# The last stage of a two-layer graph network: stores on ScalarE's queue, ten batches of x loaded ahead, statistics joined from parts

## The chip, the cores and the metric

The kernel runs on one core of a Trainium2 chip. The metric is the device time of one execution in microseconds (us), the median of three runs. A core has five engines that work side by side: TensorE (PE in the profile, with PEld for its weight loads), VectorE (DVE), ScalarE (ACT), GpSimd (POOL) and SyncE (SP). Each of them runs its own list of instructions in order, and they wait for one another by semaphores. Transfers between the device memory and the on-chip memory (DMAs) are issued by an engine and then run by themselves.

## The reference

Two layers with a residual each; everything is float32. There are 16 batches of 1024 nodes with 256 features.

```python
h = maximum(layernorm(x), 0)
x = x + layer0(h, para, adj, kv_w)      # graph weights, then attention with 4 heads
h = maximum(layernorm(x), 0)
x = x + layer1(h, adj, W1, b1, g1, be1, W2, b2, g2, be2)

def layer1(features, A, W1, b1, g1, be1, W2, b2, g2, be2):
    A_hat = (A + I) normalised by its degrees
    x   = (A_hat @ features).reshape(-1, 256)
    h   = relu(batchnorm(x @ W1.T + b1, g1, be1))   # 512 features
    out = batchnorm(h @ W2.T + b2, g2, be2)         # 256 features
    return out.reshape(16, 1024, 256)

def batchnorm(x, gamma, beta):                      # over all 16384 rows
    return (x - mean(x, 0)) * rsqrt(var(x, 0) + 1e-5) * gamma + beta
```

What matters here is the end. The second batch normalisation needs the mean and the variance of each of 256 features over all 16384 rows. So the last products have to be done, and their statistics joined, before the first value of the output can be scaled.

## The kernel before

There are two stages. Stage one does layer 0 and the first half of layer 1, batch by batch. It leaves two things in device memory: `x1_d`, the residual x of every batch, and `z1_d`, the 512 features before the first batch normalisation, as 32 tiles of 512 rows. Stage two starts at L985 and is what the change is about. It has three parts.

1. **Second linear layer (L1155 to L1243).** Each of the 32 tiles of z1 is fetched by SP (`fetch`, L145), scaled and cut at zero on ACT (`relu_on`, L134), and multiplied by W2 on PE into two blocks c of 128 features. Tiles 2 to 25 are done in pairs with seven products (`Pair`), the others plainly. The result z2 stays on chip, with the features on partitions. DVE takes the statistics of every 128x512 block with `bn_stats` into `st2` (six numbers for each block and feature). The last two tiles (30 and 31) stay in PSUM, in the four tiles of `ps_last`, and the order there is c = 0 for both tiles, then c = 1 for both.
2. **The second batch normalisation (`bn2`, L110 to L129).** `invert` joins the 32 records of a block with `bn_aggr`, adds eps on DVE, takes the power -1/2 on POOL, and adds b2 to the mean and takes it away again; `affine` makes from this the scale s and the shift t for each feature.
3. **The output loop (L1269 to L1291).** For each batch, z2 is scaled by s and t (`finish`: ACT does c = 0, DVE does c = 1), turned by 16 transposes on PE into two PSUM tiles of 128x4x256 (`ps_out` holds two), added on DVE to x of that batch (two instructions of 128x1024 at L1288), and stored (two DMAs of 512 KB, issued by POOL at L1289). The scaling of batch b+1 stands before the two additions of batch b.

The residual x comes back in two halves for each batch (`load_x1`, on SP's queue). `AHEAD = 9` batches are asked for before the loop. Batches 0 to 6 go into the pool `io`, which has 14 buffers of 4 KB per partition that the tiles of the pairs used before (tag `x1`); batches 7 and 8 go into the four buffers that hold the fetched z1 tiles 30 and 31 (pool `lasting`, tag `z`), and so have to wait for the last products. Batch b+9 is asked for at the end of turn b, into the buffers of a batch that has been stored; such a load waits for that store to land.

The order of the instructions on each engine is the order of the program (`tc.manual_schedule`). A DMA that reuses a completion semaphore waits for the earlier DMA on it; there are eight of them for the DMAs of SP and eight for those of POOL.

`st1`, the statistics of the first batch normalisation, lies in a pool that lives to the end (`const`, L90). It is read for the last time at the end of stage one (`bn1.invert(2, 4)`, L771).

Of the kernel before, what the change touches and what calls it, by code (L numbers as in the profile page):

```python
# [10 lines left out]
F32 = mybir.dt.float32  # L11
# [13 lines left out]
AHEAD = 9  # L25
# [4 lines left out]
def fast_path(  # L30
# [59 lines left out]
    st1 = const.tile([P, FC, TT, 6], F32, tag="st1", name="f_st1")  # L90
# [7 lines left out]
    class BatchNorm:  # L98
# [11 lines left out]
        def invert(self, f0, f1):  # L110
            for f in range(f0, f1):
                nc.vector.bn_aggr(
                    self.mv[:, f, :], self.st[:, f, :, :].rearrange("p t s -> p (t s)")
                )
            at = slice(f0, f1)
            nc.vector.tensor_scalar_add(self.var[:, at], self.mv[:, at, 1], EPS)
            nc.gpsimd.tensor_tensor(
                self.rstd[:, at], self.var[:, at], mhalf[:, : f1 - f0], ALU.pow
            )
            if self.offset is not None:  # L120
                mean = self.mv[:, at, 0]
                nc.vector.tensor_add(mean, mean, self.offset[:, at])
                nc.vector.tensor_sub(mean, mean, self.offset[:, at])

        def affine(self, f0, f1):
            at = slice(f0, f1)
            nc.vector.tensor_mul(self.s[:, at], self.rstd[:, at], self.gamma[:, at])
            nc.vector.tensor_mul(self.ms[:, at], self.mv[:, at, 0], self.s[:, at])
            nc.vector.tensor_sub(self.t[:, at], self.beta[:, at], self.ms[:, at])  # L129

    bn1 = BatchNorm(st1, FC, g1_t, be1_t, "bn1")
# [24 lines left out]
    with ExitStack() as stage:  # L156
# [8 lines left out]
        small = stage.enter_context(tc.tile_pool(name="fsmall", bufs=2))  # L165

# [818 lines left out]
    with ExitStack() as stage:  # L985
        big = stage.enter_context(tc.tile_pool(name="fbig2", bufs=1))
        io = stage.enter_context(tc.tile_pool(name="fio", bufs=NH * (AHEAD - 2)))

        xts = {}

        def load_x1(b, pool=None, tag="x1", bufs=None):

            xts[b] = []
            for h in range(NH):
                t = (pool or io).tile([P, NC // NH, C], F32, tag=tag, name=f"f_x1t_{b}_{h}", bufs=bufs)
                nc.sync.dma_start(t, x1_d[b].rearrange("(p h i) d -> p h i d", h=NH, p=P)[:, h])
                xts[b].append(t)

        st2 = big.tile([P, CC, TT, 6], F32, tag="st2", name="f_st2")
        with tc.manual_schedule(engines={ENG.PE, ENG.Activation, ENG.DVE, ENG.Pool, ENG.SP}):  # L1000
# [174 lines left out]
            for p in SEVEN:  # L1175
# [20 lines left out]
                else:  # L1196
# [5 lines left out]
                    for n in range(AHEAD - 2):  # L1202
                        load_x1(n)
# [14 lines left out]
                if p == SEVEN[1]:  # L1218
                    flag_out(bad)
            for n, t in enumerate(rest):  # L1220
# [12 lines left out]
            for t in range(TT - 2, TT):  # L1233
                relu_all(t)
            for c in range(CC):
                for t in range(TT - 2, TT):
                    ps = ps_last.tile([P, 512], F32, tag="last", name=f"f_z2ps_{t}_{c}")
                    product(ps, t, c, 0)
                    product(ps, t, c, 2)
                    nc.vector.bn_stats(st2[:, c, t, :], ps)  # L1240
                    last[t % 2, c] = ps
                bn2.invert(c, c + 1)
                bn2.affine(c, c + 1)  # L1243

            for b in range(AHEAD - 2, AHEAD):
                load_x1(b, lasting, "z", 4)
            ready = {}

            def finish(b, c, i0, i1):
                s, t = bn2.s[:, c : c + 1], bn2.t[:, c : c + 1]  # L1250

                def scaled(out, src):
                    if c == 0:
                        nc.scalar.activation(out, src, AF.Identity, bias=t, scale=s)
                    else:
                        nc.vector.tensor_scalar(out, src, s, t, ALU.mult, ALU.add)

                if b + 1 < B:
                    ready[b, c] = z2[:, c, b, :]
                    at = ready[b, c][:, i0 * P : i1 * P]  # L1260
                    scaled(at, at)
                else:
                    ready[b, c] = lasting.tile(
                        [P, N], F32, tag=("w2n", "w2T")[c], name=f"f_zo_{c}"
                    )
                    for g in range(NH):
                        scaled(ready[b, c][:, ts(g, 512)], last[g, c])

            for b in range(B):  # L1269
                xt = xts.pop(b)  # L1270
                out_v = out[b].rearrange("(p i) d -> p i d", i=NC)
                outs = []
                for i0 in range(0, NC, 4):
                    ps = ps_out.tile([P, 4, C], F32, tag="out", name=f"f_outps_{b}_{i0}")
                    for c in range(CC):
                        if b == 0:
                            finish(b, c, i0, i0 + 4)
                        for i in range(4):
                            nc.tensor.transpose(
                                ps[:, i, ts(c, P)], ready[b, c][:, ts(i0 + i, P)], ident  # L1280
                            )
                    outs.append(ps)
                if b + 1 < B:
                    for c in range(CC):
                        finish(b + 1, c, 0, NC)
                for i0, ps in zip(range(0, NC, 4), outs):
                    here = xt[i0 // 4]
                    nc.vector.tensor_add(here, here, ps)  # L1288
                    nc.gpsimd.dma_start(out_v[:, i0 : i0 + 4, :], here)  # L1289
# [516 lines left out]
```

## Time and profile before

| what | us |
|---|---|
| median of 3 runs (2463.08 to 2463.96) | 2463.73 |
| the profiled execution's own time | 2463.73 |
| its span, first to last instruction | 2461.9 |
| PE busy in the span | 2399.5 (97%) |
| DVE busy | 1700.3 (69%) |
| ACT busy | 1308.5 (53%) |
| last product of the second linear layer ends | about 2386.3 |
| first addition of the output loop starts | 2391.3 |
| first store is issued | 2393.2 |
| last addition ends | 2440.8 |
| last store is issued | 2447.2 |

The span is 1.8 us shorter than the time of the same execution; the difference lies around the program. All times in this document that have no other name are counted from the start of the span. The page of the whole execution shows PE busy throughout, up to the last fortieth of it or so; the part that the change touches is the last 75 us, with a few microseconds around 2185, where stage one goes over into stage two. The page's chain of waits is empty in this profile, so the end has to be read from the timelines of the single engines and from tables of windows.

In a line of the timeline stand the start, the duration, the engine, the line of the source, the operation with what it writes and reads, its shape, the number of instructions that are merged, and in brackets the idle time before it and what ended it. In a table of windows stand, for each stretch, the busy time of each engine, the clock that TensorE was granted (1.00 is full), the busy share of the DMA engines and the rate in GB/s.

### The profile page before, as it was taken

To read this page: it belongs to the slowest core of one execution; us is meant where nothing else is said; L and a number is where in the kernel's file an instruction comes from. 1 tells how busy PE (TensorE), PEld (TensorE's weight loads), DVE (VectorE), ACT (ScalarE), POOL (GpSimd) and SP (SyncE) were. 2 spreads that over 40 slices of the span, in tenths; PEclk is the share of its full clock that TensorE was granted. 3 is DMA by queue.
4 is the path that set the end of the run, shared out by engine and by line. 5 is a ranking of instruction groups with operands and counts; after the bars stand their busy time and mean duration, and the time that the engine had idled before them with its cause. 6 is when DMAs were issued, how large, how long until landed. Compare 5 with 4: busy or idle time off the path is not lost.

```text
span 2461.9 us, 24485 instructions
## 1 busy us (share of the span) xinstructions
PE 2399.5 (97%) x8062; PEld 1058.3 (43%) x8062; DVE 1700.3 (69%) x2314; ACT 1308.5 (53%) x1887; POOL 325.8 (13%) x577
## 2 busy tenths in 40 slices
PE   7999999999999999999999999999999999999984
PEld 4443444434343434444443434343444434444443
DVE  4787668584949486776859494958577586657746
ACT  7746546464646454554546364645555456246550
POOL 2030202020020302020202002030202020000002
PEclk9999999999999999999999999999999999999998
DMA  5041414222321414142322233241414220445559
GB/s 180 4 142 60 145 60 127 79 87 70 114 90 61 137 60 146 60 137 68 120 75 91 75 100 97 67 139 60 146 60 137 69 65 31 159 174 174 190 194 365
DMA packets 174424, 271.82 MB, mean 110 GB/s; under 512 B 37584, under 2 KB 121040, under 8 KB 174288
## 3 DMA queue, kind: packets, MB, share of 16 engines
q1 hardware_dynamic: 154128, 237.62, 29.7%
q0 software_dynamic: 20160, 32.55, 4.2%
q8 instruction: 66, 1.08, 0.2%
q14 instruction: 70, 0.57, 0.1%
HBM read 165.68 MB, written 70.84 MB: 96 GB/s over the span
## 4 chain that ended last, share of the span: by engine, by line


## 5 line engine op out<-in xcount | busy, mean ns | idle before, releaser
L371 ACT ACTIVATE f_p<-f_s 128x1024 f32<-128x1024 f32 x512 | 477.4, 1046 | 155.4 <-PE f_s L363 155.3
L380 DVE TENSOR_TENSOR f_acc<-f_acc,f_p 128x1024 f32<-128x1024 f32 x384 | 470.5, 1225 | 42.1 <-DVE f_acc L380 1.8
L363 PE MATMUL f_s<-f_qT,f_kT 64*128 64x512 f32 x2048 | 456.9, 596 | 0.0
L404 PE MATMUL f_o<-f_p,f_v 128*64 128x512 f32 x2048 | 453.6, 595 | 0.0
L309 PE MATMUL f_gps<-f_w,f_h_a 128*128 128x512 f32 x1024 | 446.4, 596 | 3.8 <-DVE f_w L267 3.8
L286 POOL DMA_DIRECT2D f_hT<-f_hQ x480 | 236.4, 500 | 1221.3 <-PE f_gps L309 1172.0
L363 PEld LDWEIGHTS f_s<-f_qT,f_kT 64*128 64x128 f32 x2048 | 190.6, 185 | 263.4 <-ACT f_p L371 117.2
L309 PEld LDWEIGHTS f_gps<-f_w,f_h_a 128*128 128x128 f32 x1024 | 193.4, 191 | 253.0 <-issue 231.1
L404 PEld LDWEIGHTS f_o<-f_p,f_v 128*64 128x64 f32 x2048 | 141.4, 137 | 304.4 <-issue 256.2
L267 DVE SCALAR_TENSOR_TENSOR f_w<-f_w,f_adj 128x1024 f32<-128x1024 f32 x128 | 155.0, 1213 | 54.1 <-ACT f_w L266 54.1
L263 ACT ACTIVATE f_w<-f_row,f_col 128x1024 f32<-128x1024 f32 x128 | 148.1, 1157 | 24.9 <-DMA f_row<-frow 22.1
L220 ACT ACTIVATE f_h_b<-f_x,f_shift_b,f_rstd_b 128x256 f32<-128x256 f32 x128 | 64.6, 587 | 161.5 <-DVE f_shift_b L215 161.5
L266 ACT ACTIVATE f_w<-f_w 128x1024 f32<-128x1024 f32 x128 | 135.3, 1057 | 4.1
L595 DVE TENSOR_TENSOR f_aggT<-f_u,f_aps 128x512 f32<-128x512 f32 x16 | 11.0, 688 | 182.8 <-PE f_aps L552 182.8
L552 PE MATMUL f_aps<-f_ahatT,f_hs 128*128 128x512 f32 x256 | 115.1, 592 | 0.0
L327 PE MATMUL f_kps<-f_hT,f_kvw 128*128 128x512 f32 x256 | 113.5, 593 | 1.0 <-DVE f_qT L336 0.8
L552 PE MATMUL f_aps<-f_t,f_hs 128*128 128x512 f32 x256 | 112.6, 592 | 1.6 <-DVE f_hs L546 1.6
L342 PE MATMUL f_vps<-f_kvw,f_hT 128*128 128x256 f32 x512 | 113.1, 379 | 0.0
L552 PE MATMUL f_aps<-f_ahatT,f_h_b 128*128 128x512 f32 x256 | 112.6, 592 | 0.0
L342 PEld LDWEIGHTS f_vps<-f_kvw,f_hT 128*128 128x128 f32 x512 | 97.3, 190 | 20.1 <-issue 6.0
L220 ACT ACTIVATE f_h_a<-f_x,f_shift_a,f_rstd_a 128x256 f32<-128x256 f32 x128 | 75.0, 587 | 54.4 <-DVE f_shift_a L215 54.4
L377 DVE TENSOR_TENSOR f_acc<-f_p,f_p 128x1024 f32<-128x1024 f32 x64 | 76.3, 1192 | 29.9 <-ACT f_p L371 29.9
(181 smaller groups left out, 2563.8 us busy)
## 6 DMA issues: line engine op xcount, KB each, us to landing
f_t<-ft SPq DMA_DIRECT2D x84, 512.0 KB, 7.6
f_x<-in_x_dram SPq DMA_DIRECT2D x32, 1024.0 KB, 6.0
fz<-f_z SPq DMA_DIRECT2D x64, 512.0 KB, 9.2
f_zb<-fz SPq DMA_DIRECT2D x36, 512.0 KB, 5.6
f_para<-in_L_gnn_para_dram SPq DMA_DIRECT2D x32, 512.0 KB, 4.6
f_att<-f_oT SPq DMA_DIRECT2D x512, 32.0 KB, 1.9
fx<-f_x SPq DMA_DIRECT2D x16, 1024.0 KB, 5.6
f_x1t<-fx SPq DMA_DIRECT2D x32, 512.0 KB, 6.3
```

The source lines that it names most:

```text
L220: nc.scalar.activation(self.h[:, c, :], self.xt[:, c, :], AF.Relu, bias=self.shift[:, c : c + 1], scale=self.rstd[:, c : c + 1], accum_out ...
L263: nc.scalar.activation(w, rows[b], AF.Abs, bias=cols[b][:, c : c + 1], scale=0.5 / C)
L266: nc.scalar.activation(w, w, AF.Tanh)
L267: nc.vector.scalar_tensor_tensor(w, w, 1.0, adj_t[c], ALU.subtract, ALU.mult)
L286: queue.dma_start(to[ts(k, 32), ts(a, 32 * NC)], t[ts(a, 32), k].rearrange("i c r -> i (c r)"),)
L309: nc.tensor.matmul(gps[d][:, ts(g, 512)], hs[b][:, c, ts(d, P)], w[:, ts(g, 512)], start=(c == 0), stop=(c == NC - 1),)
L342: nc.tensor.matmul(ps[:, i, :], hT[e][:, ts(c4 + i, P)], kvw_t[:, e, C : 2 * C], start=(e == 0), stop=(e == CC - 1),)
L363: nc.tensor.matmul(ps[:, e, :], kT[rows_e, pair, ts(m, P)], qT[rows_e, pair, ts(g, 512)], start=True, stop=True,)
L371: nc.scalar.activation(p, ps, AF.Exp)
L380: nc.vector.tensor_add(acc_of[s], acc_of[s], p)
L404: nc.tensor.matmul(o_of[s][e * HD : (e + 1) * HD, :], v[:, m, ts(2 * pair + e, HD)], p[:, e, :], start=(m == 0), stop=(m == NC - 1),)
L552: nc.tensor.matmul(ps, left[:, m, :], right(m), start=not more and m == 0, stop=(m == KH - 1), skip_group_check=more,)
```

## The change

Six edits, all for the end of the kernel.

- `AHEAD` is 10. The pool `io` has 15 buffers in place of 14. Batch 9 of x is asked for ahead of the loop over the last plain tiles, its first half into the buffer `w2n` (which held the sums of W2 that the pairs use), its second into `io`. Batches 7 and 8 go where they went before.
- `st1` moves from the lasting pool into stage one's own.
- For the last block (c = 1, tile 31) the product is done in two halves of 256 columns, with `bn_stats` on each, and the records of the other 31 blocks are joined ahead in two groups (`gather`), so that the last `bn_aggr` reads six triples (count, mean, sum of squares) and not 32 records.
- In `bn2`, the mean is made negative in the step that takes b2 away, and the shift comes from one instruction for each block (`scalar_tensor_tensor`) and not from two.
- In the output loop, scaling runs two batches ahead. ACT does c = 0 of every batch and c = 1 of every odd one; DVE does c = 1 of the even ones. For batch 0, the second block is scaled in halves, one on each engine. The last batch's scaled values go into `io`.
- The stores are issued by ACT's queue, each right behind its addition, and no longer by POOL's. In the built program the DMAs of ACT and SP now share one set of eight completion semaphores.

```diff
-AHEAD = 9
+AHEAD = 10
...
-        def invert(self, f0, f1):
+        def invert(self, f0, f1, triples=None):
             for f in range(f0, f1):
                 nc.vector.bn_aggr(
-                    self.mv[:, f, :], self.st[:, f, :, :].rearrange("p t s -> p (t s)")
+                    self.mv[:, f, :],
+                    self.st[:, f, :, :].rearrange("p t s -> p (t s)")
+                    if triples is None
+                    else triples,
                 )
...
-                nc.vector.tensor_sub(mean, mean, self.offset[:, at])
+                nc.vector.tensor_sub(mean, self.offset[:, at], mean)
...
+            if self.offset is not None:
+                for f in range(f0, f1):
+                    one = slice(f, f + 1)
+                    nc.vector.scalar_tensor_tensor(
+                        self.t[:, one], self.mv[:, f, 0:1], self.s[:, one],
+                        self.beta[:, one], ALU.mult, ALU.add,
+                    )
+                return
...
-        io = stage.enter_context(tc.tile_pool(name="fio", bufs=NH * (AHEAD - 2)))
+        io = stage.enter_context(tc.tile_pool(name="fio", bufs=NH * (AHEAD - 3) + 1))
...
+            load_x1(AHEAD - 1, [(lasting, "w2n", 1), (io, "x1", None)])
             for n, t in enumerate(rest):
...
+            triples = big.tile([P, 6, 3], F32, tag="triples", name="f_triples")
+            SPLIT = TT // 2
+            for k, n in enumerate((SPLIT, TT - 1 - SPLIT)):
+                nc.vector.memset(triples[:, k, 0:1], float(n * 512))
+            def gather(k, t0, t1):
+                nc.vector.bn_aggr(
+                    triples[:, k, 1:3],
+                    st2[:, CC - 1, t0:t1, :].rearrange("p t s -> p (t s)"),
+                )
+                one = triples[:, k, 2:3]
+                nc.vector.tensor_scalar_mul(one, one, float((t1 - t0) * 512))
+            gather(0, 0, SPLIT)
             for c in range(CC):
                 for t in range(TT - 2, TT):
                     ps = ps_last.tile([P, 512], F32, tag="last", name=f"f_z2ps_{t}_{c}")
...
+                    gather(1, SPLIT, TT - 1)
+                    for k in range(2):
+                        at = slice(256 * k, 256 * (k + 1))
+                        for f in range(FC):
+                            nc.tensor.matmul(ps[:, at], w2T[:, f, ts(c, P)],
+                                zs[t, f - f % 2][:, f % 2, at],
+                                start=(f == 0), stop=(f == FC - 1))
+                        nc.vector.bn_stats(
+                            triples[:, 2 + 2 * k : 4 + 2 * k, :].rearrange("p k s -> p (k s)"),
+                            ps[:, at])
...
             for b in range(B):
                 xt = xts.pop(b)
...
+                if b == 0:
+                    finish(0, 0)
+                    finish(1, 0)
+                    for h in range(NH):
+                        turn_out(0, h, 0, outs[h])
+                    ready[0, 1] = z2[:, 1, 0, :]
+                    for h in range(NH):
+                        at = ready[0, 1][:, ts(h, 512)]
+                        scaled(at, at, 1, h == 1)
+                    finish(1, 1)
+                    for h in range(NH):
+                        turn_out(0, h, 1, outs[h])
+                else:
+                    for h in range(NH):
+                        for c in range(CC):
+                            turn_out(b, h, c, outs[h])
+                soon = [(b + 2, c) for c in range(CC)] if b + 2 < B else []
+                for n in soon:
+                    if by_scalar(*n):
+                        finish(*n)
+                for h in range(NH):
+                    nc.vector.tensor_add(xt[h], xt[h], outs[h])
+                    nc.scalar.dma_start(out_v[:, 4 * h : 4 * h + 4, :], xt[h])
+                for n in soon:
+                    if not by_scalar(*n):
+                        finish(*n)
                 if b + AHEAD < B:
                     load_x1(b + AHEAD)
```

`turn_out` issues the four transposes of one half and one block; `scaled` and `finish` are as before, except for the engine that is chosen (`by_scalar(b, c)`: c == 0 or b odd).

## The prediction

> **What bounds the kernel now.** I read the windows of the last 100 us first, because the page's chain of waits is empty and PE's 97% says nothing of the end.
>
> ```profile
> 2370.00:2380.00 10.00, 9.17 (x22) 3.91 (x21) 3.82 (x6) 0.00 (x0) 0.00 (x0) 1.00 0.22 83
> 2380.00:2390.00 10.00, 6.78 (x19) 2.97 (x17) 5.83 (x18) 7.30 (x8) 1.10 (x2) 0.96 0.64 207
> 2390.00:2394.40 4.40, 4.22 (x20) 4.15 (x21) 3.89 (x6) 4.40 (x5) 0.61 (x1) 0.50 0.03 10
> 2394.40:2404.00 9.60, 7.63 (x54) 6.33 (x53) 9.39 (x10) 7.00 (x8) 2.42 (x5) 0.92 0.97 334
> 2404.00:2440.00 36.00, 24.12 (x183) 19.26 (x180) 34.74 (x36) 0.00 (x0) 11.14 (x21) 1.00 1.03 411
> 2440.00:2453.00 13.00, 0.00 (x0) 0.00 (x0) 0.78 (x1) 0.00 (x0) 3.20 (x6) 0.51 1.03 415
> 2453.00:2458.00 5.00, 0.00 (x0) 0.00 (x0) 0.00 (x0) 0.00 (x0) 0.00 (x0) 0.50 0.43 175
> 2458.00:2461.90 3.90, 0.00 (x0) 0.00 (x0) 0.00 (x0) 0.00 (x0) 0.00 (x0) 0.50 0.00 0
> ```
>
> The columns are the stretch, its length, the busy time of PE, PEld, DVE, ACT and POOL, the granted clock, the DMA share and GB/s. From 2404 to 2453 the transfers run at 411 to 415 GB/s, share 1.03, while all engines are done at 2440.8. So the output loop is bound by bytes, not by its additions. Ahead of it the transfers stand nearly idle (83, 207 and 10 GB/s), and after 2458 nothing moves. The end is therefore: first packet of a store, plus bytes over rate, plus what is lost at both edges, plus the closing.
>
> Second, DVE's timeline shows why the first store comes when it does.
>
> ```profile
> 2386.38 0.70 DVE L1240 BATCH_NORM_STATS2 f_st<-f_z2ps 128x6 f32<-128x512 f32 x1 [2.73 <-PE f_z2ps L1012]
> 2387.11 1.02 DVE L112 BATCH_NORM_AGGREGATE f_bn_mv<-f_st 128x2 f32<-128x192 f32 x1
> ...
> 2389.38 0.16 DVE L129 TENSOR_TENSOR f_bn_t<-f_be,f_bn_ms 128x1 f32<-128x1 f32 x1
> 2389.57 1.73 DVE L1256 TENSOR_SCALAR f_z<-f_z,f_bn_s,f_bn_t 128x512 f32<-128x512 f32 x3
> 2391.33 1.22 DVE L1288 TENSOR_TENSOR f_x1t<-f_x1t,f_outps 128x1024 f32<-128x1024 f32 x1
> ```
>
> The shift of c = 1 is ready at 2389.54, three scalings take DVE to 2391.3, and only then the first addition runs, to 2392.55. POOL's timeline and the rows of the closing lines come third.
>
> ```profile
> 2393.21 0.61 POOL L1289 DMA_DIRECT2D out_dram<-f_x1t  x1 [4.25 <-DVE f_x1t L1288]
> 2403.75 1.65 POOL L1289 DMA_DIRECT2D out_dram<-f_x1t  x3 [3.53 <-DVE f_x1t L1288]
> ```
>
> ```profile
> L1317 POOLq EVENT_SEMAPHORE  x5: 17/43/43, 2454.2 to 2457.2; - x5
> L1317 ACTq TENSOR_LOAD <-flag x1: 462/462/462, 2388.8 to 2388.8; - x1
> L1317 POOLq INC_SWDGE_SEM  x1: 862/862/862, 2457.3 to 2457.3; - x1
> ```
>
> ```profile
> L1801 POOLq DRAIN  x3: 46/107/2841, 2458.2 to 2461.6; - x3
> ```
>
> POOL issues 0.66 us after the addition has ended, and once sits 3.5 us. Its last semaphore of a store passes at 2457.2; then it alone goes through 0.86 and 2.84 us of closing instructions before the engines meet at 2461.1 and end at 2461.9.
>
> **The sum before.** Bytes from the first packet on are the rates by the lengths of the rows: 9.6 x 0.334 + 36 x 0.411 + 13 x 0.415 + 5 x 0.175 = 24.27 MB. At 411 GB/s that is 59.05 us. From 2394.4 to 2457.2 are 62.8, so 3.75 are lost: 1.8 in the row at 334 GB/s (9.6 x 77/411) and 1.95 at the ramp down and last landing. Closing: 4.7. This profiled execution took 2463.73, the median itself, so differences of the span can be taken from the median.
>
> **1. Statistics and the first store: -2.3.** The last bn_stats has 256 columns: 0.41 (the layer norm's 128x256 bn_stats, L205) for 0.70. The last bn_aggr reads 18 numbers: between 0.15 (L207, 6 numbers) and 1.02 (192 numbers); I take 0.2, the row that it is nearest to. One small instruction of 0.16 and its gap, 0.20, goes. The product in halves costs 8 x 0.221 (L342, 128x256) for 4 x 0.43, +0.05. The early joins (two aggregates of 96 and 90 numbers, about 0.55 each, two multiplications, two memsets) lie in DVE's idle stretches of 3.08 and 2.73 before the last statistics; without that cover they would cost 1.4. So the shift is ready 1.3 earlier, at 2388.3. Then one half's scaling (L1256 at 128x512, 0.55), a semaphore, four transposes (0.60 at full clock; I add 0.2 for a halved one) and the addition, from 2389.8 to 2391.0: 1.5 earlier. ACT's sequencer reached its flag load at 2388.8 while ACT's scalings ran to 2401.4, so it issues ahead of its engine and I let it issue at 2391.05 without POOL's 0.66. An SP store alone (L742) lands in 2.6, POOL's quickest in 3.0, so the first packet comes 0.2 sooner after its issue: 2392.1 for 2394.4. Were ACT to work off its three scalings first (0.8 + 1.1 + 1.1), the issue would be at 2391.4. Ends: -1.0 to -2.6.
>
> **2. The hole at the start: -1.3.** DVE then gives a batch (1.05 MB) each 2.35 us for two additions, plus 0.8 on every second: 0.38 MB/us, nearly the rate, and loads join when the first store has landed, 2.6 after its issue. I leave 0.5 of the 1.8 lost. Ends: 0 to -1.8.
>
> **3. Batch 9: -2.55.** Its 1.05 MB move to the 83 GB/s stretch: SP asks for it ahead of batches 7 and 8, and its second half needs the buffer of plain tile 29, freed at about 2371.6 where SP issued its last load of batch 6. 1.05/0.411 = 2.55. It is worth that only as long as the loop stays bound by bytes. DVE's work per batch falls from 2.98 to 2.7 on average, ACT's is 1.5 scalings of 1.13 and two issues of 0.35, 2.4; with a load the bytes need 5.1, alone 2.55. DVE is thus hidden while loads run and is slightly the longer in the last batches, covered by its lead.
>
> **4. The closing: -2.35.** POOL has no store to wait for, so its 0.86 and 2.84 pass long before. What follows the last landing is SP's: eight semaphores (0.5, as at 2439.5 to 2440.0), twelve more (0.8), and the meeting of the engines (0.8): about 2.35 with gaps, for 4.7. Ends: 0 (if POOL's drain stays last) to -3.
>
> **5. Where stage one ends: +0.6.** The fifteenth buffer and the moved `st1` shift addresses. In the changed SP queue the first load of the first pair, once issued at 2166.4, stands behind the last four stores of z1 and waits for them; the last is issued at 2181.4 and lands 2.6 later. Here the trace has no slack:
>
> ```profile
> 2191.45 1.52 ACT L137 ACTIVATE f_zb<-f_zb,f_bn_t,f_bn_s 128x512 f32<-128x512 f32 x2 [1.60 <-DMA f_zb<-fz]
> 2193.37 1.52 ACT L137 ACTIVATE f_zb<-f_zb,f_bn_t,f_bn_s 128x512 f32<-128x512 f32 x2 [0.41 <-DMA f_zb<-fz]
> ...
> 2194.92 1.23 DVE L1064 TENSOR_TENSOR f_zt<-f_zb,f_zb 128x1024 f32<-128x1024 f32 x1 [7.99 <-ACT f_zb L137]
> 2198.82 1.95 PE L1074 MATMUL f_zx<-f_zt,f_w2s 128*128 128x512 f32 x4
> ```
>
> ACT already waits for these loads, DVE for ACT, and PE's product at 2198.82 starts as DVE's sums end. Another 512 KB ahead of them is 1.25 us of transfers (up to 1.9 at the slower rates there), less its head start of 1.1. PE has no idle time to absorb it later. Ends: 0 to +1.9.
>
> **Waits added.** Each store on ACT waits for its addition and for the DMA that used its semaphore before: in the built order mostly the store two batches back, four at the end. Behind a held store stand the scalings of batch b+3, and PE's transposes behind those. But scaling is two batches ahead, and at least 2 MB of stores plus loads stay under way, 5 us of transfers, so no transfer waits for it.
>
> The sum is -2.3 - 1.3 - 2.55 - 2.35 + 0.6 = -7.9: **2455.8**.
>
> The Trainium skill (DMA: Bandwidth & Descriptors, Issuing engines are not separate DMA queues) speaks against the move of the stores: all issuers share the same 16 engines, and a second issuer saves only issue time. The rows agree on rate (411 mixed, 415 for POOL alone). By the rule alone, terms 2 and 4 would be nothing and the sum 2459.5; I keep them, since they are POOL's stall and POOL's closing, not bandwidth.
>
> **Rivals.**
> - *POOL's drain stays last.* The 2.84 us may follow the end of all stores, whoever issues them: 2455.8 + 2.35 = 2458.2. For it: it is the last thing in the trace. Against: it follows POOL's own 0.86 directly.
> - *The seam costs more.* If the pair's load also waits for PE, all four loads shift by a whole load and more: 1.9 and a second product late, 2457.1 to 2459.
> - *Batch 9 isn't early.* If its buffers come free only with the last products, term 3 is gone: 2458.3. Against: SP's last load of batch 6 went out at 2371.6.
> - *Slower: ACT's queue starves the stores.* If the shared semaphores let only one batch be under way, a pair of batches needs landing 2.6 + scalings 2.3 + transposes 2.1 + addition 1.2 = 8.2 for 5.1 us of bytes; over the last five pairs that is 3.1 x 5 = 15.5: 2471. It decides once fewer than about 0.9 MB (2 us) are in flight.
>
> **Chances.** Forecast 0.62 (its own range 2453.5 to 2457.8), drain 0.12, seam 0.10, batch 9 0.06, ACT starving 0.06, the rest unnamed. The range of 8 in 10 is 2453.0 to 2460.0: the low end has every term near its better bound, the high one two terms lost. This kernel's measurement can tell 0.2%, 4.9 us: below 2458.8 is faster. That holds for the forecast, most of the drain and batch 9 cases and half the seam: 0.80; within 0.12; slower 0.08.
>
> **What would show it.** First store issued by ACT near 2391 (plus the seam's delay), a rate above 400 GB/s from 2 us later without a break, no load of batch 9 after 2380, and under 3 us from the last landing to the end. At the seam, the idle time before PE's product at 2198.8 gives term 5. I am wrong if the rate falls below 390 with both hardware queues, if ACT's stores wait long on semaphores with DMA idle, or if the drain of 2.84 still ends the span.

## The result, and the profile after

The changed kernel takes 2458.47 us in the median of 17 runs (2456.13 to 2461.64), the kernel before 2463.96 in 17 runs beside them (2462.04 to 2468.91): a ratio of 0.9976, with a 95% interval of 0.9969 to 0.9983. So it is faster, by 5.5 us where 7.9 were forecast, and inside the range of 2453.0 to 2460.0. The profiled execution took 2456.69, with a span of 2454.9; that is 7.0 less than the span before.

The windows of the end of the changed kernel, with the columns as before:

```profile
2370.00:2380.00 10.00, 9.17 (x22) 3.85 (x21) 4.49 (x10) 0.00 (x0) 0.00 (x0) 1.00 0.36 127
2380.00:2387.00 7.00, 6.47 (x25) 4.21 (x24) 3.70 (x11) 2.37 (x2) 0.55 (x1) 1.00 0.48 147
2387.00:2392.00 5.00, 2.35 (x20) 1.88 (x18) 3.65 (x10) 2.96 (x3) 0.55 (x1) 1.00 0.61 215
2392.00:2404.00 12.00, 9.59 (x74) 7.67 (x73) 11.77 (x12) 7.36 (x7) 0.00 (x0) 1.00 0.91 329
2404.00:2440.00 36.00, 21.49 (x136) 17.97 (x135) 23.52 (x23) 16.12 (x15) 0.00 (x0) 0.81 1.03 418
2440.00:2446.00 6.00, 4.13 (x32) 3.26 (x31) 5.55 (x5) 1.13 (x2) 0.00 (x0) 1.00 1.03 419
2446.00:2453.00 7.00, 0.00 (x0) 0.00 (x0) 0.00 (x0) 0.00 (x0) 0.00 (x0) 0.65 0.60 241
2453.00:2455.00 2.00, 0.00 (x0) 0.00 (x0) 0.00 (x0) 0.00 (x0) 0.00 (x0) 0.50 0.00 0
```

The transfers still set the end: 418 GB/s from 2404 on, without a break. DVE and PE are less busy in that stretch than before, and this costs nothing. From 2370 to 2380 the rate is 127 and not 83: that is batch 9. The first 12 us of the stores are still at 329 GB/s; that hole was to close and did not. ACT issues the first store at 2391.59:

```profile
2391.59 1.47 ACTq L1359 DMA_DIRECT2D out_dram<-f_x1t  x2
```

To see where the 7.0 us came from, both profiled executions are cut at the same events (the first and last packet are those of the stores in the trace's DMA records):

| piece | before | after | difference | forecast |
|---|---|---|---|---|
| start to stage one's last product (PE) | 2166.11 | 2164.76 | -1.35 | 0 |
| from there to the first pair's product that reads DVE's sums | 32.71 | 33.91 | +1.20 | +0.6 |
| from there to the start of the last plain tiles' products | 173.55 | 173.55 | 0 | 0 |
| from there to the first addition of the output | 18.96 | 18.12 | -0.84 | -1.5 |
| first addition to first packet of a store | 3.07 | 2.13 | -0.94 | -0.8 |
| first to last packet | 62.21 | 59.70 | -2.51 | -1.3 - 2.55 |
| last packet to end of the span | 5.29 | 2.73 | -2.56 | -2.35 |

Of what the change touches, only the place of `st1` lies in the time of the first row. In the 14 profiled executions of this study that product starts between 2164.6 and 2167.5, and in the 12 of them that have `st1` moved it starts at 2166.1 in the mean, as in the kernel before. So 1.35 us of the gain in the spans are chance. The spans are given to 0.1 us, so the last row, and the last column in the table of experiments, are good to about 0.05. The other rows sum to -5.65, which agrees with the medians' -5.5.

The measured -5.65 falls short of the forecast's -7.9 by 2.25: 0.6 at the seam, where stage one goes over into stage two, 0.66 ahead of the first addition, 1.34 between the packets, and 0.35 the other way in the two rows left.

PE's timeline of the changed kernel shows what came in ahead of the first addition:

```profile
2382.59 1.89 PE L1282 MATMUL f_z2ps<-f_z,f_w2T 128*128 128x256 f32 x8
2385.01 1.99 PE L1282 MATMUL f_z2ps<-f_z,f_w2T 128*128 128x256 f32 x8 [0.53 <-DVE f_triples L1289]
2386.84 1.04 PE L1325 MATMUL f_outps<-f_ident,f_z 128*128 128x128 f32 x8
```

and DVE's timeline of the same kernel:

```profile
2384.52 0.43 DVE L1289 BATCH_NORM_STATS2 f_triples<-f_z2ps 128x6 f32<-128x256 f32 x1 [0.24 <-PE f_z2ps L1282]
2387.04 0.43 DVE L1289 BATCH_NORM_STATS2 f_triples<-f_z2ps 128x6 f32<-128x256 f32 x1 [2.09 <-PE f_z2ps L1282]
2387.50 0.24 DVE L111 BATCH_NORM_AGGREGATE f_bn_mv<-f_triples 128x2 f32<-128x18 f32 x1
...
2388.79 0.22 DVE L133 SCALAR_TENSOR_TENSOR f_bn_t<-f_bn_mv,f_bn_s,f_be 128x1 f32<-128x1 f32 x1
2389.04 0.55 DVE L1309 TENSOR_SCALAR f_z<-f_z,f_bn_s,f_bn_t 128x512 f32<-128x512 f32 x1
2390.34 2.35 DVE L1358 TENSOR_TENSOR f_x1t<-f_x1t,f_outps 128x1024 f32<-128x1024 f32 x2 [0.75 <-PE f_outps L1325]
```

The durations are those forecast (0.43 for 0.41, 0.24 for 0.2). What is new is the bracket on PE's second line: the second half of the product did not start behind the first, but waited for DVE to have read the first half. A wait took the place of the one removed.

The rows of the two closing lines, first L1390 and then L1874, of the changed kernel:

```profile
L1390 SPq EVENT_SEMAPHORE  x8: 17/17/17, 2452.7 to 2453.2; - x8
L1390 POOLq INC_SWDGE_SEM  x1: 2651/2651/2651, 2393.3 to 2393.3; - x1
```

```profile
L1874 SPq EVENT_SEMAPHORE  x14: 17/28/28, 2453.3 to 2454.8; - x14
L1874 POOLq DRAIN  x3: 46/107/10109, 2395.9 to 2454.6; - x3
```

POOL's own closing instruction and its long drain begin at 2393.3 and 2395.9 and are over by 2406, while stores still run. Behind the last landing only SP's semaphores and the meeting of the engines are left.

ACT's waits from 2390 to 2452 (who waited for what, us in total, times, longest) show the held stores:

```profile
ACT f_z L1307 <- DVE f_x1t L1358: 15.5, 8, 4.2
ACT f_z L1307 <- DMA f_x1t<-fx: 5.8, 1, 5.8
```

ACT's scalings stood 21.3 us behind stores that waited. Of these, about 18.5 us lie after 2404, where the rate is 418 GB/s, so no transfer waited for them.

### The profile page after: what moved, and what is told of

It reads as the page before. It is cut to its first block, busy times and chain, and to the rows that moved or that the text cites. A ratio compares the mean times of both kernels' runs of the same rounds, so it can differ in the third digit from the quotient of the medians.

```text
span 2454.9 us, 24503 instructions
## 1 busy us (share of the span) xinstructions
PE 2399.2 (98%) x8070; PEld 1060.6 (43%) x8070; DVE 1693.8 (69%) x2309; ACT 1319.9 (54%) x1896; POOL 307.8 (13%) x545
## 4 chain that ended last, share of the span: by engine, by line
PE 94%; DVE 2%; DMA 2%; ACT 1%; issue 1%; POOL 0%; ACTq 0%; SPq 0%; DVEq 0%; POOLq 0%
PE f_s L379 18%; PE f_o L420 18%; PE f_gps L325 17%; PE f_aps L568 15%; PE f_zps L663 6%; PE f_vps L358 5%; PE f_kps L343 4%; PE f_zx L1092 3%; PE f_zm L1092 2%; PE f_z2ps L1030 2%; DVE f_x1t L1358 1%; PE f_zps L744 1%; PE f_zps3b L663 0%; PE f_zps3a L663 0%; ACT f_h_a L236 0%
```

## The experiments

Times are medians; each ratio stands against the kernel before on the same chip. "Addition to last packet" runs from the start of the first addition to the store's last packet: 65.28 before, 61.83 in the changed kernel.

| run | edit of | median (runs) | ratio, 95% interval | addition to last packet | last packet to end |
|---|---|---|---|---|---|
| changed kernel | | 2458.47 (17) | 0.9976 (0.9969, 0.9983) | 61.83 | 2.73 |
| e1_seam | changed | 2457.05 (7) | 0.9970 (0.9958, 0.9981) | 61.59 | 2.74 |
| e2_whole | changed | 2458.64 (10) | 0.9977 (0.9967, 0.9986) | 62.96 | 2.74 |
| e3_order | changed | 2457.82 (8) | 0.9976 (0.9965, 0.9986) | 62.31 | 2.58 |
| e4_pool | changed | 2462.45 (11) | 0.9993 (0.9984, 1.0002) | 62.04 | 5.16 |
| e5_no9 | changed | 2460.14 (11) | 0.9985 (0.9976, 0.9995) | 62.98 | 2.71 |
| e6_noload | changed | 2443.98 (5) | 0.9917 (0.9903, 0.9931) | 47.19 | 2.34 |
| e7_zo | changed | 2458.19 (9) | 0.9980 (0.9970, 0.9990) | 61.70 | 2.69 |
| e8_later | changed | 2458.55 (10) | 0.9979 (0.9969, 0.9988) | 61.42 | 2.62 |
| e9_dve | changed | 2458.71 (9) | 0.9979 (0.9969, 0.9989) | 61.23 | 2.75 |
| e10_best | changed | 2455.46 (5) | 0.9966 (0.9952, 0.9979) | 61.59 | 2.64 |
| e11_act | before | 2461.59 (11) | 0.9990 (0.9981, 0.9999) | 65.24 | 2.69 |
| e12_again | changed | 2456.51 (7) | 0.9969 (0.9958, 0.9980) | 61.87 | 2.65 |

Medians that differ by 1 us can hardly be told apart; where it matters the verdict goes by pieces of the trace. A piece of a single profile varies too: in the ten profiles of the changed loop with batch 9 early, the addition-to-last-packet time lies between 61.2 and 63.0, with a mean of 61.85.

### The closing and the issuer: e4_pool and e11_act

e4_pool undoes one part of the change, e11_act makes that part alone in the kernel before:

```diff
-                    nc.scalar.dma_start(out_v[:, 4 * h : 4 * h + 4, :], xt[h])
+                    nc.gpsimd.dma_start(out_v[:, 4 * h : 4 * h + 4, :], xt[h])
```

> The changed kernel, with the stores issued by POOL again and all else as changed. If POOL's closing was what the change took off the end: 0.86 and about 2.8 us of POOL stand again behind the last landing, from the last packet to the end of the span it is 5.0 to 5.4 us (2.7 in the changed kernel), the first packet comes 0.6 to 0.9 later after its addition, and the median is 2.5 to 4 higher, 2461 to 2462.5. Rival, that the shorter end came from something else (SP's or ACT's closing): the end stays at about 2.7 us and the median within 1 us of 2458.5.

> The kernel before with one edit: the stores of the output loop are issued by ACT's queue. If the closing and the issue are POOL's own, this part alone gives 2.4 us at the end (5.3 to about 2.8 from the last packet to the end of the span) and 0.7 to 0.9 at the first packet: median 2464.0 - 3.2 = 2460.8. Rival, that ACT's scaling of c = 0, which stands between the stores there, holds the stores up: the rate from 12 us on falls below 405 GB/s and the gain shrinks to 1.5 or less, 2462.5.

With POOL the rows of the two closing lines of e4_pool are again those of the kernel before:

```profile
L1390 POOLq INC_SWDGE_SEM  x1: 862/862/862, 2453.9 to 2453.9; - x1
```

```profile
L1874 POOLq DRAIN  x3: 46/107/2841, 2454.8 to 2458.2; - x3
```

From the last packet to the end it is 5.16 us with POOL and 2.73 with ACT; in e11_act it falls from 5.29 to 2.69. So the closing is worth 2.4 to 2.6 us, and the change of issuer alone brings it. The rival of something else at SP or ACT is out. The medians put e4_pool 4.0 us above the changed kernel, 3.45 when each is taken against the kernel before beside it; with the width of the intervals this does not contradict the pieces.

The other half of the expectation is open. The first packet comes 3.07 us after the first addition has started with POOL (both kernels) and 2.13 with ACT (both): 0.94 sooner, as forecast. But from that addition to the *last* packet it is 62.04 with POOL and 61.83 with ACT in the changed loop, 65.28 and 65.24 in the old one. So of the 0.94 us by which the stores start sooner, these two pairs of profiles show 0.0 and 0.2 at the end; as the same loop varies by 1.8 us from profile to profile, they can't exclude that the whole of it arrives. e11_act's gain of 2.0 us in the medians is no more than the closing. ACT's scaling, its rival, did not hold the stores up either: the rate of e11_act is

```profile
2404.00:2440.00 36.00, 20.92 (x121) 18.77 (x122) 23.69 (x24) 9.92 (x8) 0.00 (x0) 0.76 1.02 415
```

### The hole after the first store: e6_noload, e7_zo, e8_later

The forecast put the hole down to DVE's pace and let scaling ahead close most of it. e6_noload leaves the loop's loads out (batches 10 to 15 add what the buffers of batches 0 to 5 hold):

```diff
-                xt = xts.pop(b)
+                xt = xts[b % AHEAD]
...
-                if b + AHEAD < B:
-                    load_x1(b + AHEAD)
```

> The changed kernel without the six loads of x inside the loop: batches 10 to 15 add what lies in the buffers of batches 0 to 5, so their output is another. It asks what makes the hole after the first store (215 and 285 GB/s in the second and third stretch of 2 us after the first packet, where the stores of batch 1 are issued in time but move 3 us later). If the first loads that join make it: without them the stores of batch 1 move 0.9 to 1.2 us after their issue, and no stretch of the first 8 us is under 370 GB/s. Rival, that DVE's additions or ACT's queue do not deliver fast enough: the second and third stretch stay under 300. The whole then ends after 16.8 MB at 0.38 to 0.415 MB/us, 40 to 44 us after the first packet: 2437 to 2443.

The first four stretches of 2 us after the first packet, in the changed kernel:

```profile
2392.50:2394.50 2.00, 1.30 (x10) 0.86 (x8) 2.00 (x4) 1.39 (x2) 0.00 (x0) 1.00 1.02 414
2394.50:2396.50 2.00, 1.81 (x15) 1.63 (x16) 1.88 (x3) 1.40 (x2) 0.00 (x0) 1.00 0.74 213
2396.50:2398.50 2.00, 1.67 (x14) 1.24 (x13) 2.00 (x3) 0.83 (x1) 0.00 (x0) 1.00 0.87 287
2398.50:2400.50 2.00, 1.15 (x12) 0.94 (x11) 2.00 (x3) 1.54 (x2) 0.00 (x0) 1.00 1.03 352
```

and in e6_noload:

```profile
2394.70:2396.70 2.00, 1.33 (x11) 0.86 (x8) 2.00 (x4) 1.36 (x2) 0.00 (x0) 1.00 1.02 412
2396.70:2398.70 2.00, 1.78 (x15) 1.60 (x16) 1.88 (x3) 1.39 (x2) 0.00 (x0) 1.00 0.82 336
2398.70:2400.70 2.00, 1.66 (x14) 1.24 (x13) 2.00 (x3) 0.86 (x1) 0.00 (x0) 1.00 1.03 420
2400.70:2402.70 2.00, 1.15 (x11) 0.94 (x10) 2.00 (x3) 1.91 (x2) 0.00 (x0) 1.00 0.99 404
```

DVE, PE and ACT do the same work in both tables, stretch by stretch; what differs is the last column. Against 415 GB/s the changed kernel loses (202 + 128 + 63) x 2 / 415 = 1.9 us in its second to fourth stretch. (The kernel before had 373, 268, 260 and 365 in the same places: 1.9 again.) Without the loads 0.4 are left, in the second stretch, which is short of stores: it stays under the 370 expected of it. So the first loads that join make the larger part of the hole, 1.5 us in this pair of profiles, and DVE's pace the smaller. In the changed kernel the second batch's first store is issued at 2394.57, with the first load issued at 2394.46, and its packets start at about 2397.4; from 2395.5 to 2397.5 the load runs alone at 195 GB/s. In e6_noload the same store is issued at 2396.81 and its packets start at 2397.68. The size of the hole varies: in the other profiles with loads in the loop the first 8 us lose between 0.9 us (e4_pool, where loads and stores move side by side and the next 4 us lose 0.8 more) and 2.2 us (e2_whole).

Without loads the loop as a whole takes 45.05 us from the first to the last packet for 16.87 MB, 1 us over the expectation's upper end. Then it is DVE that is full, as this window of e6_noload shows, and the rate is below 415:

```profile
2405.00:2436.00 31.00, 23.31 (x176) 18.65 (x175) 29.86 (x28) 17.28 (x17) 0.00 (x0) 1.00 0.96 388
```

If the loads cost so much because they come early, they should come later. e7_zo took the last batch's two buffers out of `io` ahead of the loop, so that batch 10 should get those of batch 1:

```diff
+            zo = [io.tile([P, N], F32, tag="x1", name=f"f_zo_{c}") for c in range(CC)]
...
-                    ready[b, c] = io.tile([P, N], F32, tag="x1", name=f"f_zo_{c}")
+                    ready[b, c] = zo[c]
```

> The changed kernel, with the two buffers of the last batch's scaled values taken from `io` ahead of the loop: they get the buffers of batch 0, and batch 10 waits for the store of batch 1 in place of batch 0's, so that every load of the loop starts one batch later. If the joining loads cost bandwidth only because few stores are under way when they come: the hole moves to 4 to 8 us after the first packet and is smaller, 59.7 us from the first to the last packet become 58.2 to 59.0, and the median is about 1 us lower, 2457.5. Rival, that the loads cost the same whenever they join: 59.4 to 60 us, and 2458.5.

That edit moved nothing: SP's queue and its waits came out as in the changed kernel, the first load still waiting for batch 0's store. It serves as a second measurement of the changed kernel, 2458.19 for 2458.47. e8_later touches the two buffers, and there the load does wait:

```diff
+                if b == 0:
+                    zo += [io.tile([P, N], F32, tag="x1", name=f"f_zo_{c}") for c in range(CC)]
+                    for c in range(CC):
+                        nc.gpsimd.memset(zo[c][:, 0:1], 0.0)
-                if b + AHEAD < B:
-                    load_x1(b + AHEAD)
+                elif b + AHEAD - 1 < B:
+                    load_x1(b + AHEAD - 1)
```

> The changed kernel, with the two buffers of the last batch's scaled values taken at the end of turn 0 and touched there by POOL (one column set to 0), and batch b+9 asked for at the end of turn b from turn 1 on: the first load of the loop (batch 10) now really waits for batch 1's store, some 2.5 us later than batch 0's. If the joining loads cost bandwidth only because few stores are under way when they come: the hole moves to 5 to 8 us after the first packet and is smaller, 59.7 us from the first to the last packet become 58.2 to 59.0, and the median is about 1 us lower, 2457.5. Rival, that the loads cost the same whenever they join: 59.2 to 60 us, and 2458 to 2459.

The stretches of 2 us after the first packet in e8_later:

```profile
2393.90:2395.90 2.00, 1.32 (x11) 0.86 (x8) 2.00 (x4) 1.37 (x2) 0.00 (x0) 1.00 1.03 424
2395.90:2397.90 2.00, 1.79 (x15) 1.61 (x16) 1.88 (x3) 1.39 (x2) 0.20 (x2) 1.00 0.80 328
2397.90:2399.90 2.00, 1.66 (x15) 1.24 (x13) 2.00 (x3) 0.86 (x1) 0.00 (x0) 1.00 1.09 418
2399.90:2401.90 2.00, 1.15 (x11) 0.94 (x10) 2.00 (x3) 1.91 (x2) 0.00 (x0) 1.00 0.99 260
2401.90:2403.90 2.00, 1.80 (x15) 1.35 (x13) 1.88 (x3) 1.39 (x2) 0.00 (x0) 1.00 0.86 291
```

The hole went with the loads, from the second and third stretch to the fourth and fifth. It is not clearly smaller: these five stretches lose 1.7 us, the first five of the changed kernel 1.9 and of e7_zo 1.3. From the first to the last packet it takes 59.27 us, against 59.70 and e7_zo's 59.58, and the median is 2458.55. As far as one profile can tell, the rival holds: the loads cost about the same whenever they join. The pattern is not the same, though: here the stores slow down first, to 246 and 188 GB/s in the two half microseconds from 2400.0, before a packet of a load has moved, and then the loads run almost alone. Why the stream stalls when loads join is open.

### Batch 9: e5_no9

```diff
-            load_x1(AHEAD - 1, [(lasting, "w2n", 1), (io, "x1", None)])
...
-                if b + AHEAD < B:
-                    load_x1(b + AHEAD)
+                if b + AHEAD - 1 < B:
+                    load_x1(b + AHEAD - 1)
```

> The changed kernel, with batch 9 of x asked for inside the loop again, at the end of turn 0 (and `io` with 14 buffers). If the loop is bound by bytes and batch 9 was worth its transfer: 24.2 MB move from the first store's packet on in place of 23.2, from the first to the last packet it takes 62.2 us in place of 59.7, and the median is 2.5 higher, 2461.0. Rival, that something else sets the loop's length now (ACT's held stores, DVE), so that the early load is hidden anyway: 59.7 us and 2458.5 stay.

24.25 MB move from the first packet on in place of 23.19, as expected. The median rises by 1.7 us, and the addition-to-last-packet time by 1.15, to 62.98, which is at the upper end of the ten profiles with batch 9 early (61.2 to 63.0). So the early load is worth something, more likely 1 to 2 us than 2.55, and one profile can't say which. What the same run does show is the loop's own part. It moves the same bytes as the kernel before, with the new order of scaling, in 62.98 us for 65.28.

### Who scales: e9_dve

```diff
-                return c == 0 or b % 2 == 1
+                return c == 0
```

> The changed kernel, with the scaling of c = 1 on DVE for every batch (ACT keeps c = 0, and half of batch 0's c = 1). If the loop is bound by bytes from about 10 us on, the division of the scaling is worth nothing there: 59.2 to 60.2 us from the first to the last packet, median 2458 to 2459. Rival, that DVE becomes the bound in the last batches (2.35 + 0.8 us for each against 2.5 us of bytes): the rate falls below 400 GB/s in the last 15 us and the end comes 2 to 3 us later, 2461.

59.09 us from the first to the last packet, and 2458.71: moving every second scaling of c = 1 to ACT is worth nothing that can be seen. The rate in the last stretch, 2437 to 2450, is 418 GB/s, so DVE is not the bound there either.

### The last product: e2_whole and e3_order

e2_whole does the last product whole, with one `bn_stats` of 512 columns. e3_order keeps the halves, and puts tile 30 between them:

```diff
+                if c + 1 == CC:
+                    half(0)
+                    product(last[0, c], TT - 2, c, 0)
+                    product(last[0, c], TT - 2, c, 2)
+                    nc.vector.bn_stats(st2[:, c, TT - 2, :], last[0, c])
+                    gather(1, SPLIT, TT - 1)
+                    half(1)
```

> The changed kernel, with the last product done whole again and one bn_stats of 512 columns on it; the early joins stay. If the second half waited for the bn_stats of the first because both lie in one PSUM tile: no idle time of 0.53 us on PE inside the last products; from the start of the last tile's product to the shift of c = 1 it takes 5.9 us in place of 6.4 (PE 0.85 earlier, bn_stats 0.27 longer), and the first store is 0.5 earlier. Rival, that the halves pay as they stand (the wait is hidden by something later): the shift comes 0.2 to 0.3 us later, 6.6 to 6.7. The median can hardly tell: 2458.0 or 2458.7.

> The changed kernel, with the order of the last three products turned: first half of tile 31, then all of tile 30, then the second half of tile 31 (all for c = 1). The bn_stats of the first half then runs under tile 30's product. If the wait for that bn_stats was the loss: PE has no idle time in the last products, and from the start of c = 1's first product to its shift it takes about 9.05 us, against 9.86 in the changed kernel; the median is 0.8 lower, 2457.7. Rival, that DVE is now late (bn_stats of tile 30, 0.70, and the second join, 0.71, stand between): 9.4 or more, and no gain against the whole product.

PE's timeline of e3_order:

```profile
2380.42 1.89 PE L1282 MATMUL f_z2ps<-f_z,f_w2T 128*128 128x256 f32 x8
2382.15 3.60 PE L1030 MATMUL f_z2ps<-f_z,f_w2T 128*128 128x512 f32 x8
2385.58 1.89 PE L1282 MATMUL f_z2ps<-f_z,f_w2T 128*128 128x256 f32 x8
```

No bracket is left. From the start of the last plain tiles' products to the first addition it is 18.96 us before, 18.12 in the changed kernel, 17.55 with the whole product (2374.35 to 2391.90) and 17.33 with the turned order (2373.48 to 2390.81). So the halves lost 0.57 against what they replaced, and pay 0.22 once their wait is covered. Both rivals are out. As expected, the medians can't show it.

### The seam: e1_seam, e10_best, e12_again

```diff
-        io = stage.enter_context(tc.tile_pool(name="fio", bufs=NH * (AHEAD - 3) + 1))
+        one = stage.enter_context(tc.tile_pool(name="fone", bufs=1))
+        io = stage.enter_context(tc.tile_pool(name="fio", bufs=NH * (AHEAD - 3)))
...
-            load_x1(AHEAD - 1, [(lasting, "w2n", 1), (io, "x1", None)])
+            load_x1(AHEAD - 1, [(lasting, "w2n", 1), (one, "x1one", None)])
```

e10_best and e12_again are one kernel: this edit and e3_order's.

> The changed kernel, with the fifteenth buffer in a pool of its own ahead of the other fourteen, so that the first pair's first load stands ahead of the last four z1 stores in SP's queue again, as before the change. If the seam lost 1.2 us because that load stood behind the stores: PE's first product of the first pair starts after 0.0 to 0.2 us of idle time (1.18 in the changed kernel), everything from there on is 1.0 to 1.2 us earlier against the end of stage one, and the median falls from 2458.5 to about 2457.4. Rival, that ACT's work or the rate of the transfers there is what came late: the idle time stays at about 1.2 us and the median at 2458.5.

> The changed kernel with two of the earlier edits together: the fifteenth buffer in a pool of its own (the first pair's load again ahead of the last z1 stores) and the last products in the order half, tile 30, half. If both losses were real and add: from the start of the last product of stage one to the first product of the first pair that reads DVE's sums 32.7 to 33.2 us (32.7 before, 33.9 changed), no idle time in the last products, and the median 0.8 + 0.7 lower than the changed kernel's 2458.5: 2457.0. Rival, that the seam is chance and not the queue's order: 33.5 to 34.2 us there, and 2457.7.

> The kernel with both edits (fifteenth buffer in a pool of its own; last products in the order half, tile 30, half) once more, since its first median (2455.5, five runs) lies 1.5 us lower than the two edits explain. If the two losses are all there is: a median of 2456.5 to 2457.3, and 32.5 to 33.2 us from the start of stage one's last product to the first pair's product that reads DVE's sums. Rival, that the fifteenth buffer's own pool brings something more: 2455.5 again.

SP's timeline of the changed kernel at the seam:

```profile
2169.73 10.62 SPq L758 DMA_DIRECT2D fz<-f_z  x4
2182.78 0.32 SPq L162 DMA_DIRECT2D f_zb<-fz  x1
```

and of e10_best:

```profile
2166.73 0.32 SPq L162 DMA_DIRECT2D f_zb<-fz  x1
2171.41 10.62 SPq L758 DMA_DIRECT2D fz<-f_z  x4
```

`f_zb<-fz x1` is the pair's first load: behind the four stores in the one, ahead of them in the other. PE's timeline of the changed kernel, and then of e10_best, has the product that reads DVE's sums:

```profile
2198.67 1.96 PE L1092 MATMUL f_zx<-f_zt,f_w2s 128*128 128x512 f32 x4 [1.18 <-DVE f_zt L1087]
```

```profile
2199.01 1.88 PE L1093 MATMUL f_zx<-f_zt,f_w2s 128*128 128x512 f32 x4
```

One profile would not settle it, since the time from stage one's last product to this one varies. With the load ahead of the stores it is 32.71 (before), 33.22 (e1_seam), 32.58, 32.57 and 32.59 (e10_best, e11_act, e12_again): 32.7 in the mean of five. With the load behind them, in the changed kernel and its eight other edits, it lies between 32.82 and 34.19, in the mean of nine 33.6. Single profiles of the two groups overlap; by the means the order in the queue costs 0.9 us. The fifteenth buffer by itself is not what turned the order: e5_no9 has fourteen again, and there too the first load (issued at 2185.33) stands behind the four stores (from 2172.28). What e5_no9 keeps is `st1` in its new place, and the small tile of the triples; neither was undone alone. In e1_seam a buffer ahead of `io` turns the order back. e1_seam's own idle time there was still 0.49 where 0.0 to 0.2 were expected, half a miss, though its median of 2457.05 is near the 2457.4 expected.

e10_best and e12_again together have a median of 2456.0 in 12 runs, 2.4 below the changed kernel and 1.7 by the pieces (0.9 and 0.79). That they add is shown; that there is more in it is not, since their intervals overlap with the changed kernel's. It is the fastest version of this study.

## Why the prediction was right, and where not

The direction and the bound were right: bytes set the end, and the gain came from the edges. The time lies inside the range because the range left room for two lost terms: 2.25 us were lost, spread over three terms. Of the four signs that were named, three came (the first store issued near 2391, no load of batch 9 after 2380, under 3 us behind the last landing); the rate above 400 GB/s from 2 us later on did not, with 213, 287 and 352 in the next stretches. Step by step:

1. **Statistics and the first store (-2.3).** The step that failed is "the product in halves costs 8 x 0.221 for 4 x 0.43, +0.05": it counted the work of the halves and not the wait between them, which took 0.79 back (e3_order). The rest of the count was right: without that wait the first addition starts 1.63 earlier, for 1.5 forecast. The Trainium skill (Perfetto Trace Analysis, Matmuls) says that independent groups of products should rotate through PSUM banks, so that the reading of one overlaps the next; the two halves lie in one tile, and the 0.53 us on PE agree. The other part, 0.8 for the issue and the start, was measured at 0.94 and is real at the first packet; e4_pool and e11_act show 0.0 to 0.2 of it at the last, in one pair of profiles each, so how much of it arrives is open.
2. **The hole (-1.3).** The rate by itself did not improve: 1.9 us are lost in the first 8 us in both kernels. The step that failed is the reason given, DVE's pace; most of the hole, 1.5 of the 1.9 us, is loads that join (e6_noload), and they cost about the same later (e8_later). Counted from the first addition, though, the new loop is 2.3 us shorter for the same bytes (e5_no9 against before, one profile). So the issue and the hole together, 2.1 in the forecast, came out, but as one gain: two terms were written for it, and how it divides between them isn't shown. The scaling on ACT has no part in it that can be seen (e9_dve); that leaves the scaling two batches ahead and the halves of batch 0, which no run undid alone.
3. **Batch 9 (-2.55).** The mechanism is right: its halves were issued at 2368.4 and 2371.5, and 1.05 MB fewer move in the loop. The size was most likely too large: 1.1 us in the trace, 1.7 in the medians (e5_no9), each uncertain by about a microsecond. Why bytes that are gone should not be worth their full transfer is open.
4. **The closing (-2.35).** Right: -2.56, shown both ways at 2.43 (e4_pool) and 2.60 (e11_act). The rival of the drain that stays last is out. So is the sum by the rule alone: the Trainium skill (DMA: Bandwidth & Descriptors, Issuing engines are not separate DMA queues) lets a second issuer save only issue time. For the rate it holds nearly; for the end of the program it doesn't, since 2.4 us of the old issuer's closing go with it.
5. **The seam (+0.6).** The mechanism is right, the size was 0.9 (1.20 in the profiled pair). The prices named for it, a load of 1.25 to 1.9 us less a head start of 1.1, give 0.15 to 0.8; the 0.6 was picked from among them, and even the upper end is below what was measured. That the fifteenth buffer has a part in it is not shown (e5_no9).

Of the waits added, "no transfer waits for it" held: 18.5 us of ACT's waits after 2404, and 418 GB/s. The rival of ACT's queue starving the stores did not come.

## What to carry to other kernels

When a loop is bound by bytes, count the bytes behind its start and the closing behind its end. An earlier first transfer need not reach the end of a stream, so measure to the last packet too. A product cut in two inside one PSUM tile waited between its halves for the engine that reads the first (0.53 us here); put other work between them. Moving a tile or adding one can reorder a queue far away, so compare the order of every queue before and after.

## What the runs showed of the hardware

- The first loads that join a stream of stores can stall it. In the changed kernel they run alone at 195 GB/s for 2 us, and in the kernel before at 199, while stores that have been issued stand still. In e4_pool loads and stores move side by side from the start, so the pattern is not fixed, and it does not follow from the issuer of the stores.
- The rate of the mixed stream does not tell the two issuers apart. From 2404 to 2440 it is 411 GB/s before and 405 in e4_pool (stores from POOL), and 418 in the changed kernel and 415 in e11_act (stores from ACT), but in the two runs with POOL that stretch begins inside the hole: 299 GB/s from 2404.4 to 2406.4 before, 293 from 2404.3 to 2406.3 in e4_pool. From 2408 to 2440 it is 417 and 413 with POOL, 418 and 417 with ACT, and 406 with ACT in e3_order.
- The start of the same product ahead of the change varies by 2.9 us over 14 profiled executions. The granted clock moves single executions too. In e1_seam a stretch in which PE was busy throughout took 132.4 us (from 2209.91 to 2342.35) for 130.75 in the changed kernel. The whole difference lies in the first two groups of products behind 1.98 us of idle time: they take 5.23 us at a mean granted clock of 0.67, against 3.54 us at 1.00 in the changed kernel. The first lines are e1_seam's, the last two the changed kernel's:

```profile
2209.91 2.72 PE L1093 MATMUL f_zm<-f_zt,f_w2T 128*128 128x512 f32 x4 [1.98 <-DVE f_z L1107]
2212.42 2.88 PE L1093 MATMUL f_zm<-f_z,f_w2T 128*128 128x512 f32 x4
```

```profile
2209.47 1.98 PE L1092 MATMUL f_zm<-f_zt,f_w2T 128*128 128x512 f32 x4 [1.98 <-DVE f_z L1106]
2211.29 1.88 PE L1092 MATMUL f_zm<-f_z,f_w2T 128*128 128x512 f32 x4
```

Spans of single executions of this kernel can't tell 1 us; pieces between the same two events can do better, when the clock in them is the same.
